# Quarter-block products inside one of seven half-block products, in the LSTM steps and in layer 3's second weights

## The chip, the cores and the metric

The kernel runs on one core of a Trainium2 chip. The core has five engines that run their own queues: TensorE (matrix products, written to the eight banks of PSUM), VectorE, ScalarE, GpSimd and SyncE. In the profile they are called PE (with PEld for TensorE's weight loads), DVE, ACT, POOL and SP. The metric is the device time of one execution in microseconds (us): 2432.9 us is the median of three runs of the kernel before.

## The reference

The input x has 128 batches of 64 nodes with 256 features, in float32. Four graph layers follow, each with a layer norm, a rectifier and a residual. Two of them matter here.

Layer 0 ends with four LSTMs. For p = 1 to 4 the 64 nodes are cut into windows of p nodes; an LSTM of p steps runs over every window, and its last state replaces the last node of the window:

```python
def step(carry, x_t):
    h, c = carry
    g = x_t @ Wih.T + h @ Whh.T + bias
    i, f, gg, o = jnp.split(g, 4, axis=-1)
    c = jax.nn.sigmoid(f) * c + jax.nn.sigmoid(i) * jnp.tanh(gg)
    h = jax.nn.sigmoid(o) * jnp.tanh(c)
    return ((h, c), None)
...
for p in range(1, MAX_SKIP + 1):
    nw = Tv // p
    wins = h[:, :nw * p, :].reshape(Bv * nw, p, Hd)
    last = _lstm_last(Wih[p - 1], Whh[p - 1], bih[p - 1], bhh[p - 1], wins)
    idx = jnp.arange(nw) * p + (p - 1)
    h = h.at[:, idx, :].set(last.reshape(Bv, nw, Hd))
```

Layer 3 is three graph convolutions with weights of 256x512 (W1), 512x1024 (W2) and 1024x256 (W3):

```python
h = jax.nn.relu(_slconv(x, adj, S, W1))
h = jax.nn.relu(_slconv(h, adj, S, W2))
return _slconv(h, adj, S, W3)
```

## The kernel before

All data are float32. The 8192 tokens are worked on in 16 groups (g) of 512. Layer 0 keeps its features in four tiles `hs`, transposed, and the residual x of the first four groups stays in the tiles `xs[0]` to `xs[3]` from the start of the kernel until layer 1.

Most large products are made by the scheme that is called `seven` (L172). Weights A and data B are each cut into 2x2 blocks. Eight block products would make the result; this scheme (Strassen's, in Winograd's form) needs seven, with sums of the blocks of A (`sums`, L219, s1 to s4) and differences of the blocks of B (`differences`, L210, t1 to t4). `sevens` (L243) names the pairs: product 1 is a11 b11, 2 is a12 b21, 3 is s4 b22, 4 is a22 t4, 5 is s1 t1, 6 is s2 t2, 7 is s3 t3. `seven` issues products 1, 5, 6, 7 into four banks (`ps`), copies products 1 and 5 to SBUF (`p1`, `p5`, L181 and L182 on ScalarE), adds product 6 to p1 and product 7 to p5 (L184 and L185 on VectorE), and returns `finish`. That one sums p1 and p5 on GpSimd (L189, the block 1,1), issues product 2 on top of product 1 (block 0,0 straight from the bank), product 3 on top of 5 (block 0,1, L195) and product 4 on top of 7 (block 1,0, L199). `end` applies the activation to each block.

In the LSTM (`next_step`, L701) a unit is n = nk x 32 columns in two blocks, so blocks of B are 256 columns wide for p = 1, 2 and 4 and 224 for p = 3. Contraction runs over x and h (the two rows of blocks, 256 features each, two chunks of 128), and a block of A holds 128 of the 256 rows of each gate. One step has two gate sets: i and g, then f and o. Each gate set is one `seven`; one of its products is 2 gates x 2 chunks = 4 matmuls (L592). Two units (`two`) are worked on in turn. The first step of a window (`first_steps`, L650) has no h and is made by `gate_set` too; step t = 1 and later are `next_step`. The pairs of units are counted by j; pair j = 2 of p = 4 is the last of the LSTM, and beside its steps the results are turned and stored to DRAM (`turn_nodes`, on SP), added to the residual by GpSimd's adding transfers (`add_turned`), and layer 1 begins with `ln_relu(xs[0], h)`. The weights' sums for one p are made by `blocks_of` (L736) on VectorE, at the first pair; `ss[1]` is s2.

In layer 3, `second_weights` (L1582) multiplies the mixed features (512) by W2 (1024 columns out): for q = 0 and 2 one `seven` each, whose products are 2 x 2 matmuls (L1599) of 256 columns. Both are started before either is finished. `s2s[1]` is s2 of W2, and `m1`'s differences are `ts`. The loop over g is at L1719. `third_weights` (L1627, L1649) has blocks of 128 columns.

The order within an engine's queue is not the program's order. The framework lists the instructions by priority, which is program order, and when it builds the kernel it plans when each one's inputs will be there; an instruction that is not expected to be ready is passed by a later one of the same engine that is. `tc.issue_after` keeps single instructions behind others. On the chip the queues run in the order so fixed, and wait on semaphores.

Of the kernel before, what the change touches and what calls it, by code (L numbers as in the profile page):

```python
# [39 lines left out]
def adj_preln_kernel(ctx: ExitStack, tc: tile.TileContext, x_in, adj, vec, bg0, bg1,  # L40
# [9 lines left out]
    def bank(shape=(P, 512)):  # L50
        return psp.tile(list(shape), F32, tag="ps", name="ps")
# [119 lines left out]

    def seven(products, banks, p1, p5, out, end, parts=lambda b: [b]):  # L172

        ps = banks
        for i, p in zip((1, 5, 6, 7), ps):
            products[i](p, True)  # L180
        nc.scalar.copy(p1, ps[0])  # L181
        copied = nc.scalar.copy(p5, ps[1])  # L182

        nc.vector.tensor_tensor(p1, p1, ps[2], ALU.add)  # L184
        added = nc.vector.tensor_tensor(p5, p5, ps[3], ALU.add)  # L185

        def finish():
            sums_on_pool.append(
                nc.gpsimd.tensor_tensor(out=out[1][1], in0=p1, in1=p5, op=ALU.add).ins  # L189
            )  # L190
            end(1, 1, None)
            products[2](ps[0], False)
            end(0, 0, ps[0])
            products[3](ps[1], False)
            nc.vector.tensor_tensor(out[0][1], p1, ps[1], ALU.add)  # L195
            end(0, 1, None)
            products[4](ps[3], False)
            for to, p, q in zip(*(parts(b) for b in (out[1][0], p1, ps[3]))):
                last = nc.vector.tensor_tensor(to, p, q, ALU.add)  # L199
                end(1, 0, None, to)  # L200
            return last.ins

        finish.behind = added.ins
        finish.copied = copied.ins
        return finish

    def each_behind(behind, i):
# [108 lines left out]
    with tc.tile_pool(name="lw", bufs=5) as lw:  # L316
# [242 lines left out]
        with tc.tile_pool(name="back", bufs=1, reuse_waits="tile") as back_pool, \  # L559
# [19 lines left out]
            def by_chunk(blocks):  # L579
                return [[b[:, c] for c in range(2)] for b in blocks]  # L580

            def gate_set(p, n, g, gates, w, bs):

# [16 lines left out]
                out = [[g[:, :, m, blk, 0:n] for blk in range(2)] for m in range(2)]  # L600
                p15 = lp.tile([P, 2, 2, 256], F32, tag="p15", name="p15")
                same = gates[0][1:] == gates[1][1:]
# [5 lines left out]
                def end(m, blk, ps, part=None):  # L608
# [8 lines left out]
                return seven(  # L617
                    {i: product(i) for i in range(1, 8)}, [bank((P, 2, 256))[:, :, 0:n] for _ in range(4)],
                    p15[:, 0, :, 0:n], p15[:, 1, :, 0:n], out, end,
                )  # L620
# [79 lines left out]

            def next_step(t, p, n, u, ws, last_sum=None):  # L701

# [12 lines left out]
                if last_sum is not None:  # L715
                    last_sum()
                b = (by_chunk([x1]) + [None], by_chunk([h1, h2]), by_chunk(ts))
                ig, fo = gate_tile(), gate_tile()
                gate_i, gate_g, gate_f, gate_o = (g[:, r, :, :, 0:n] for g in (ig, fo) for r in range(2))
                gate_set(p, n, ig, [(0, 0, AF.Sigmoid), (1, 2, AF.Tanh)], ws, [b] * 2)()  # L720
                nc.vector.tensor_tensor(gate_i, gate_i, gate_g, ALU.mult)
                gate_set(p, n, fo, [(0, 1, AF.Sigmoid), (1, 3, AF.Sigmoid)], ws, [b] * 2)()
                nc.vector.tensor_tensor(cell, cell, gate_f, ALU.mult)
# [12 lines left out]
            def blocks_of(p, wi, wh):  # L736
# [11 lines left out]

                make(range(3))
                ws = [by_chunk([wx[:, m], wm[:, m]]) for m in range(2)] + [by_chunk(ss)]  # L750
                return ws, lambda: make([3])

# [3 lines left out]
                w_next[0], lw.tile([P, 2, 1024], F32, tag="w", name="s"), copied_of[5:9]  # L756
            )
            for p, nk in ((1, 8), (2, 8), (3, 7), (4, 8)):
                n = nk * HB
# [6 lines left out]
                for j in range(0, len(units), 2):  # L766
                    two = [unit(p, *u, nk) for u in units[j : j + 2]]
                    first_steps(p, n, two, units[j : j + 2], w0)
                    if p > 1:
                        flush()  # L770
                        if j == 0:
                            ws, last_sum = blocks_of(p, wi, wh)
                    if j + 2 == len(units):
# [5 lines left out]
                        else:  # L779
# [8 lines left out]
                            nc.vector.tensor_tensor(ss[1], ss[0], wqk[0][0], ALU.subtract)  # L788
                            nc.vector.tensor_tensor(wdiff, wqk[0][0], wqk[1][0], ALU.subtract)
                    for t in range(1, p):  # L790
                        for i, u in enumerate(two):
                            stepped_before = stepped
                            stepped = next_step(
                                t, p, n, u, ws, last_sum if (j, t, i) == (0, 1, 0) else None
                            )
# [785 lines left out]

    def second_weights(m1, room):  # L1582

# [6 lines left out]
        ts = [tt[:, i] for i in range(4)]  # L1590
        last = differences(nc.vector, *act[0], *act[1], *ts)

        def products(q):
# [16 lines left out]
        for q in (0, 2):  # L1610
# [6 lines left out]
                    products(q), [bank((P, 2, HN)) for _ in range(4)], p1, p5, blocks,  # L1617
                    ends_in(blocks, AF.Relu),
                )
# [95 lines left out]

    AHEAD = 4
    a, finish_start = first_start()
    s3, scaled = None, None
    for g in range(NG + 1):  # L1719
# [32 lines left out]
        if g < NG:  # L1752
            h2, behind = second_weights(m1, h1)
            if g == 0:
# [71 lines left out]
```

## Time and profile before

| what | value |
|---|---|
| time, median of 3 runs (lowest to highest) | 2432.9 us (2431.64 to 2433.43) |
| the profiled execution: its own time, and its span from the first to the last instruction | 2432.54 us, 2430.8 us |
| granted TensorE clock in it | 0.999 |
| L592 (LSTM products), records of TensorE | 5012, from 156.9 us to about 1200 us |
| L1599 (layer 3, second weights), records of TensorE | 1792, from 1680.6 us to 2413 us |
| stretch 880 to 960 us (p = 4): busy us of 80 on PE, DVE, ACT, POOL | 80.0, 48.8, 35.3, 10.4 |
| stretch 640 to 720 us (p = 3): the same | 80.0, 49.2, 38.3, 10.7 |
| stretch 1680 to 1760 us (layer 3): the same | 80.0, 50.9, 26.8, 10.4 |

A row of the timeline gives start, length, engine, line and operation, what is written and read (by tile name), the shape, and how many like instructions were merged; in brackets stands how long the engine was idle before, and who ended it. The product of the seven can be told by its operands: "h,w" is product 1, "diff,s" are 5, 6 and 7, "state,w" is 2, "state,s" is 3 and "diff,w" is 4. A float32 matmul leaves two records on PE and two on PEld. Neighbouring matmuls overlap, so the length of a merged run is the starts' distance plus the latency of its last record.

### The profile page before, as it was taken

What the parts mean: (1) busy time and instruction counts of PE and PEld (TensorE: products, weight loads), DVE (VectorE), ACT (ScalarE), POOL (GpSimd) and SP (SyncE); (2) the same over time, 40 slices, a digit from 0 to 9 for tenths busy, and PEclk for the clock granted to TensorE, in tenths of its full rate; (3) what the DMA queues carried; (4) which work ended last, traced back from release to release, by engine and by line L of the source; (5) the groups of instructions that cost most, each with busy time, mean ns of one, the idle gap of its engine ahead of it and who ended that gap; (6) DMA issues with size and microseconds to landing.
All of it is one profiled execution on the core that took longest, in us unless ns stands there. A gap on an engine that the chain in (4) does not pass through costs nothing.

```text
span 2430.8 us, 46867 instructions
## 1 busy us (share of the span) xinstructions
PE 2409.7 (99%) x19648; PEld 2088.7 (86%) x19648; DVE 1546.7 (64%) x2829; ACT 1130.2 (46%) x2022; POOL 497.5 (20%) x445
## 2 busy tenths in 40 slices
PE   9999999999999999999999999999999999999999
PEld 6778888889999998888888867586988898999898
DVE  6768866666566575575599888576655445444543
ACT  4557755444445343353455565564343333333332
POOL 4432211111111111112224445123111111111100
PEclk9999999999999999999999999999999999999999
DMA  4200000001000000143246410010233100000000
GB/s 140 84 2 1 1 18 1 1 1 35 1 1 1 1 1 1 18 96 70 48 82 129 78 29 2 10 61 10 36 53 62 27 10 19 10 10 11 18 10 19
DMA packets 161587, 73.21 MB, mean 30 GB/s; under 512 B 104416, under 2 KB 157792, under 8 KB 161376
## 3 DMA queue, kind: packets, MB, share of 16 engines
q1 hardware_dynamic: 147984, 57.08, 9.5%
q0 software_dynamic: 12672, 12.58, 3.5%
q8 instruction: 154, 2.52, 0.4%
q10 hardware_dynamic: 720, 0.56, 0.1%
q14 instruction: 57, 0.47, 0.1%
HBM read 40.84 MB, written 20.97 MB: 25 GB/s over the span
## 4 chain that ended last, share of the span: by engine, by line
PE 92%; DVE 5%; ACT 2%; issue 1%; DMA 0%; POOL 0%; ACTq 0%; DVEq 0%; POOLq 0%
PE ps L592 41%; PE ps L1599 16%; PE ps L1649 8%; PE ps L1556 4%; PE ps L146 4%; PE ps L952 3%; PE ps L501 2%; PE ps L527 2%; PE ps L1326 2%; PE ps L878 2%; PE ps L911 2%; PE ps L1388 1%; PE ps L974 1%; PE ps L1670 1%; PE ps L1354 1%
## 5 line engine op out<-in xcount | busy, mean ns | idle before, releaser
L592 PE MATMUL ps<-diff,s 128*128 128x256 f32 (+1 forms) x1824 | 393.5, 371 | 0.9 <-DVE diff L713 0.9
L1599 PE MATMUL ps<-arena 128*128 128x256 f32 x1792 | 391.4, 380 | 0.0
L1599 PEld LDWEIGHTS ps<-arena 128*128 128x128 f32 x1792 | 338.9, 190 | 48.2 <-issue 2.0
L592 PEld LDWEIGHTS ps<-diff,s 128*128 128x128 f32 x1824 | 345.9, 190 | 33.8 <-issue 1.6
L606 ACT ACTIVATE gates<-gates,lbias 128x512 f32<-128x512 f32 (+5 forms) x426 | 244.1, 620 | 200.5 <-DVE gates L195 144.8
L189 POOL TENSOR_TENSOR gates<-p 128x512 f32<-128x512 f32 (+1 forms) x115 | 148.6, 1292 | 882.0 <-DVE p L185 831.1
L592 PE MATMUL ps<-h,w 128*128 128x256 f32 (+1 forms) x1028 | 241.0, 371 | 0.0
L592 PE MATMUL ps<-diff,w 128*128 128x256 f32 (+1 forms) x1040 | 238.7, 370 | 0.0
L189 POOL TENSOR_TENSOR arena<-arena 128x512 f32<-128x512 f32 (+1 forms) x80 | 91.1, 1139 | 613.7 <-DVE arena L185 601.4
L592 PEld LDWEIGHTS ps<-diff,w 128*128 128x128 f32 x1040 | 197.4, 190 | 18.2
L592 PEld LDWEIGHTS ps<-h,w 128*128 128x128 f32 x1028 | 195.0, 190 | 19.2 <-issue 0.5
L606 ACT ACTIVATE gates<-ps,lbias 128x256 f32<-128x256 f32 (+3 forms) x213 | 91.8, 477 | 247.2 <-PE ps L592 247.0
L239 ACT ACTIVATE arena<-arena 128x512 f32<-128x512 f32 x144 | 88.5, 628 | 250.4 <-POOL arena L189 163.1
L195 DVE TENSOR_TENSOR gates<-p,ps 128x512 f32<-128x512 f32 (+1 forms) x115 | 76.3, 664 | 114.3 <-PE ps L592 114.0
L1649 PE MATMUL ps<-arena 128*128 128x128 f32 x1280 | 148.4, 275 | 0.0
L1649 PEld LDWEIGHTS ps<-arena 128*128 128x128 f32 x1280 | 146.5, 192 | 0.9
L184 DVE TENSOR_TENSOR arena<-arena,ps 128x512 f32<-128x512 f32 (+1 forms) x80 | 48.2, 602 | 138.5 <-PE ps L1599 50.0
L195 DVE TENSOR_TENSOR arena<-arena,ps 128x512 f32<-128x512 f32 (+1 forms) x80 | 48.1, 602 | 125.5 <-PE ps L1599 57.6
L228 DVE TENSOR_TENSOR arena<-arena 128x512 f32<-128x512 f32 (+1 forms) x192 | 108.2, 597 | 21.9 <-ACT arena L239 20.2
L592 PE MATMUL ps<-state,w 128*128 128x256 f32 (+1 forms) x512 | 116.1, 370 | 0.9 <-ACT p L181 0.8
L184 DVE TENSOR_TENSOR p<-p,ps 128x512 f32<-128x512 f32 (+1 forms) x131 | 86.9, 663 | 47.4 <-PE ps L592 46.6
L199 DVE TENSOR_TENSOR gates<-p,ps 128x512 f32<-128x512 f32 (+1 forms) x115 | 76.6, 666 | 62.9 <-PE ps L592 62.4
(219 smaller groups left out, 4127.1 us busy)
## 6 DMA issues: line engine op xcount, KB each, us to landing
x<-in_x SPq DMA_DIRECT2D x19, 512.0 KB, 4.1
y<-turned SPq DMA_DIRECT2D x64, 128.0 KB, 3.7
v<-vt SPq DMA_DIRECT2D x128, 64.0 KB, 2.3
w<-in_wih SPq DMA_DIRECT2D x4, 1024.0 KB, 8.4
x_for_h<-in_x SPq DMA_DIRECT2D x8, 512.0 KB, 6.6
x<-y POOLq DMA_DIRECT2D x8, 512.0 KB, 6.3
x_for_h<-y POOLq DMA_DIRECT2D x8, 512.0 KB, 6.8
z<-w SPq DMA_DIRECT2D x64, 64.0 KB, 2.0
```

Source lines behind the costliest of these rows:

```text
L146: last = nc.tensor.matmul(pss[b][half * 64 : half * 64 + 64, c, t, :], lhsT=src[rows, t, col : col + 64], rhs=a2[rows, :], start=True, sto ...
L184: nc.vector.tensor_tensor(p1, p1, ps[2], ALU.add)
L189: nc.gpsimd.tensor_tensor(out=out[1][1], in0=p1, in1=p5, op=ALU.add).ins
L195: nc.vector.tensor_tensor(out[0][1], p1, ps[1], ALU.add)
L199: last = nc.vector.tensor_tensor(to, p, q, ALU.add)
L228: last = eng.tensor_tensor(out=s, in0=p, in1=q, op=op)
L239: nc.scalar.activation(o, o, func)
L592: nc.tensor.matmul(ps[:, r], lhsT=wc[:, j, :], rhs=bc, start=first and r == 0 and c == 0, stop=True, skip_group_check=True,)
L606: nc.scalar.activation(o, ps, func, bias=lbias[:, col : col + 1])
L1556: nc.tensor.matmul(ps[:, t, :], lhsT=w[:, t * P : (t + 1) * P], rhs=b, start=first and t == 0, stop=True, skip_group_check=True,)
L1599: nc.tensor.matmul(ps[:, r, :], lhsT=w[:, c, col : col + P], rhs=b[:, c, :], start=first and r == 0 and c == 0, stop=c == 1, skip_group_ch ...
L1649: nc.tensor.matmul(ps[:, t, :], lhsT=w[:, c, t * P : (t + 1) * P], rhs=b[:, c, :], start=first and t == 0 and c == 0, stop=c == 3, skip_gr ...
```

## The change

Product 6 (s2 t2) of a `seven` may be handed a `Split`. Then s2 and t2 are themselves cut into 2x2 blocks, quarter sums and quarter differences are made of them, and the product is made by the same scheme at half the size: seven products of quarters, each one matmul of half the columns, where there were four matmuls. Products 1, 5, 7 and 6 of the quarters go to the four quarters of the bank (`first`). `common` reads them: ScalarE copies quarter 0 to u, VectorE adds quarter 3 to u and quarters 1 and 2 to the last quarter of p1, and GpSimd adds u to the last three quarters of p1. Then `last` issues products 2, 3 and 4 of the quarters on top of quarters 0, 1 and 2 of the bank, and `rest` adds those to p1 on VectorE. The add of the whole of product 6 to p1 falls away.

The split is used in every `next_step` but those of p = 4, j = 2 (both gate sets, for p = 2, 3, 4), and in `second_weights` of the groups g = 3 to 15 (both q). The quarter sums of weights are made in `blocks_of` once for each p, and by `split_second` once at g = 2; the quarter differences are made once a step, and once a group.

The room for this in the LSTM is taken from the tiles of x0 to x3: they are freed after layer 0's first use, and x is loaded into them again from DRAM at the start of pair j = 2 of p = 4. In layer 3 two of these tiles are taken again after their groups are done. The banks and p15 of a gate set are laid out without a gap when n = 224.

```diff
     def seven(products, banks, p1, p5, out, end, parts=lambda b: [b], split=None):
...
         for i, p in zip((1, 5, 6, 7), ps):
-            products[i](p, True)
+            if i == 6 and split:
+                split.first(p)
+            else:
+                products[i](p, True)
         nc.scalar.copy(p1, ps[0])
         copied = nc.scalar.copy(p5, ps[1])
-
-        nc.vector.tensor_tensor(p1, p1, ps[2], ALU.add)
-        added = nc.vector.tensor_tensor(p5, p5, ps[3], ALU.add)
+        if split:
+            split.common(ps[2], p1)
+            split.last(ps[2])
+            added = nc.vector.tensor_tensor(p5, p5, ps[3], ALU.add)
+            split.rest(ps[2], p1)
+        else:
+            nc.vector.tensor_tensor(p1, p1, ps[2], ALU.add)
+            added = nc.vector.tensor_tensor(p5, p5, ps[3], ALU.add)
...
+    class Split:
+        def __init__(self, w, b, u):
+            (a11, a12), (_, a22), ss = w
+            (b11, _), (b21, b22), ts = b
+            self.m = (
+                None, (a11, b11), (a12, b21), (ss[3], b22), (a22, ts[3]),
+                (ss[0], ts[0]), (ss[1], ts[1]), (ss[2], ts[2]),
+            )
+            self.u = u
...
+        def issue(self, to, i, first=False):
+            w, b = self.m[i]
+            nc.tensor.matmul(to, lhsT=w, rhs=b, start=first, stop=True, skip_group_check=True)
+        def first(self, ps):
+            _, q = self.quarters(ps)
+            for k, i in enumerate((1, 5, 7, 6)):
+                self.issue(q[k], i, k == 0)
+        def last(self, ps):
+            _, q = self.quarters(ps)
+            for k, i in enumerate((2, 3, 4)):
+                self.issue(q[k], i)
+        def common(self, ps, to):
+            _, q = self.quarters(ps)
+            flat, t = self.quarters(to)
+            nc.scalar.copy(self.u, q[0])
+            nc.vector.tensor_tensor(self.u, self.u, q[3], ALU.add)
+            for k in (1, 2):
+                nc.vector.tensor_tensor(t[3], t[3], q[k], ALU.add)
+            h = self.u.shape[-1]
+            three = flat[:, h : 4 * h].rearrange("p (i n) -> p i n", n=h)
+            nc.gpsimd.tensor_tensor(
+                out=three, in0=three, in1=self.u.unsqueeze(1).to_broadcast([P, 3, h]), op=ALU.add
+            )
+        def rest(self, ps, to):
+            h = self.u.shape[-1]
+            (flat, _), (pf, _) = self.quarters(to), self.quarters(ps)
+            nc.vector.tensor_tensor(flat[:, 0 : 3 * h], flat[:, 0 : 3 * h], pf[:, 0 : 3 * h], ALU.add)
+    def split_differences(eng, t, ts):
...
+        eng.tensor_tensor(
+            out=ts[:, 0:3:2], in0=t[:, :, h:], in1=t[:, 0].rearrange("p (k n) -> p k n", n=h),
+            op=ALU.subtract,
+        )
+        eng.tensor_tensor(out=ts[:, 1], in0=b[1][1], in1=ts[:, 0], op=ALU.subtract)
+        eng.tensor_tensor(out=ts[:, 3], in0=b[1][0], in1=ts[:, 1], op=ALU.subtract)
...
                 if last_sum is not None:
                     last_sum()
+                splits = [None] * 2
+                if within:
+                    s2, sw, room = within
+                    half = n // 2
+                    tb = split_differences(
+                        nc.vector, ts[1],
+                        room[:, 0:2].rearrange("p a (i n) -> p (a i) n", i=2)[:, :, 0:half],
+                    )
...
-                gate_set(p, n, ig, [(0, 0, AF.Sigmoid), (1, 2, AF.Tanh)], ws, [b] * 2)()
+                gate_set(p, n, ig, [(0, 0, AF.Sigmoid), (1, 2, AF.Tanh)], ws, [b] * 2, splits[0])()
...
-                gate_set(p, n, fo, [(0, 1, AF.Sigmoid), (1, 3, AF.Sigmoid)], ws, [b] * 2)()
+                gate_set(p, n, fo, [(0, 1, AF.Sigmoid), (1, 3, AF.Sigmoid)], ws, [b] * 2, splits[1])()
...
                 make(range(3))
+                sw = split_sums[p % 2]
+                sums(
+                    nc.vector, *(ss[1][:, c, 2 * r : 2 * r + 2] for r in range(2) for c in range(2)),
+                    *(sw[:, i] for i in range(4)),
+                )
...
+            free = [xpool.tile([P, GT, D], F32, tag=f"x{g}", name=f"free{g}") for g in range(NK)]
+            split_sums = [f.rearrange("p a (i f) -> p a i f", f=P) for f in free[:2]]
...
+                    if p == 4 and j == 2:
+                        for g in range(NK):
+                            xs[g] = xpool.tile([P, GT, D], F32, tag=f"x{g}", name=f"x{g}")
+                            load_x(xs[g], g)
                     for t in range(1, p):
                         for i, u in enumerate(two):
                             stepped_before = stepped
                             stepped = next_step(
                                 t, p, n, u, ws, last_sum if (j, t, i) == (0, 1, 0) else None,
+                                None if p == 4 and j == 2 else (*within, free[2 + i]),
                             )
...
+    SPLIT_FROM = 3
+    within = None
...
-            h2, behind = second_weights(m1, h1)
+            h2, behind = second_weights(m1, h1, within)
+            if g == SPLIT_FROM - 1:
+                with tc.issue_after(behind):
+                    within = split_second()
```

## The prediction

> **What bounds the kernel.** I read the page's busy line and its chain that ended last first: they say which engine has to become shorter.
>
> ```profile
> span 2430.8 us, 46867 instructions
> ...
> PE 2409.7 (99%) x19648; PEld 2088.7 (86%) x19648; DVE 1546.7 (64%) x2829; ACT 1130.2 (46%) x2022; POOL 497.5 (20%) x445
> ...
> PE 92%; DVE 5%; ACT 2%; issue 1%; DMA 0%; POOL 0%; ACTq 0%; DVEq 0%; POOLq 0%
> ```
>
> TensorE is busy 99% of the span and is 92% of the chain. L592 (the LSTM's products) alone is 41% of that chain and L1599 (layer 3's second weights) 16%: the two places that the change touches. So time is gained only by less TensorE work, and every wait that the change puts on TensorE costs its full length.
>
> Next, the pace of TensorE by the width of a product, from the timeline. A float32 product appears as two matmul records, so the pace is per record: the run's length less one record's own latency (379, 353 and 275 ns, from the rows of single records), over the records but one.
>
> ```profile
> 904.77 5.34 PE L592 MATMUL ps<-diff,s 128*128 128x256 f32 x24
> ...
> 597.66 4.70 PE L592 MATMUL ps<-diff,s 128*128 128x224 f32 x24
> ...
> 1848.34 5.52 PE L1649 MATMUL ps<-arena 128*128 128x128 f32 x48
> ```
>
> That is (5.34 − 0.379)/23 = 215.7 ns at 256 columns, (4.70 − 0.353)/23 = 189.0 ns at 224, and (5.52 − 0.275)/47 = 111.6 ns at 128. From 256 to 224 columns the step is 26.7 ns, 0.834 ns per column. At that slope 128 columns would take 109.0 ns; the row says 111.6. Half as wide is thus a little more than half as long.
>
> **TensorE's own work.** One half-block product (number 6 of the seven) is four matmuls of full width, 8 records; it becomes seven quarter products, 14 records of half width.
>
> Count of the splits: an LSTM step has two gate sets, each with one split. p = 2 has 4 pairs of units × 1 step × 2 = 8 steps, p = 3 has 3 × 2 × 2 = 12, p = 4 has 3 × 2 = 6 in its first pair, as the second is excluded. That is 28 splits of 256 columns (p = 2 and 4) and 24 of 224 (p = 3). Layer 3 splits in groups 3 to 15, 13 × 2 = 26, at 256 columns.
>
> - 54 splits of 256 columns: 8 × 215.7 = 1726 ns become 14 × 111.6 = 1562 ns, 163 ns less each: **−8.8 us**.
> - 24 splits of 224: before, 8 × 189.0 = 1512 ns. After, 14 records of 112 columns, which no row shows. The bounds are the 128-column pace, 14 × 111.6 = 1562 ns (+50 ns each, +1.2 us in all), and the column slope carried on, 111.6 − 16 × 0.834 = 98.3 ns, 1376 ns (−136 ns each, −3.3 us). I take +1.2: the 128-column row lies above its own slope, which is what a floor under the record would look like, and it is the nearest row.
>
> The two say −7.6 us with a range of −12.1 to −7.6. Every record has its own weight load, 14 in place of 8 now, and at 128 columns the loads fill the time as well: L1649's 1280 loads are busy 146.5 us, 114 ns each.
>
> [...]
>
> **The new wait.** The last three quarter products add into the bank whose first four must have been read: by one ScalarE copy (u), one VectorE add into u and two into the last quarter of p1. In the first gate set of a step that fits:
>
> ```profile
> 927.21 1.89 PE L592 MATMUL ps<-h,w 128*128 128x256 f32 x8
> 928.94 5.34 PE L592 MATMUL ps<-diff,s 128*128 128x256 f32 x24
> 929.62 1.23 DVE L721 TENSOR_TENSOR gates<-gates 128x1024 f32<-128x1024 f32 x1 [1.52 <-ACT gates L606]
> 930.87 0.59 ACT L182 COPY p<-ps 128x512 f32<-128x512 f32 x1 [0.87 <-PE ps L592]
> 932.66 0.69 DVE L184 TENSOR_TENSOR p<-p,ps 128x512 f32<-128x512 f32 x1 [1.82 <-PE ps L592]
> ```
>
> Products 5, 6, 7 are the x24. With the split, 5 ends at 928.94 + 1.73 = 930.67, the four quarters at 931.56, product 7 at 933.29. Prices of the reads: a VectorE add from a bank takes 683 ns at 512 columns and 420 at 256 (rows of L184), so 0.29 us at 128 and 0.55 at 384; a ScalarE copy 0.58 and 0.37 (L181), so 0.26 at 128. A reader starts some 0.25 us after the last record's end by pace (L184 at 932.66 against 932.39). So u is copied 931.8 to 932.1, VectorE adds until 933.0, and product 7 still runs until 933.3: no wait, by 0.3 us. VectorE has nothing else there.
>
> The second gate set is different:
>
> ```profile
> 941.03 5.34 PE L592 MATMUL ps<-diff,s 128*128 128x256 f32 x24
> 942.30 1.23 DVE L724 TENSOR_TENSOR state<-state,gates 128x1024 f32<-128x1024 f32 x1
> 943.62 1.06 ACT L625 ACTIVATE gates<-state 128x1024 f32<-128x1024 f32 x1
> 944.71 1.23 DVE L627 TENSOR_TENSOR state<-gates 128x1024 f32<-128x1024 f32 x1 [1.18 <-ACT gates L625]
> 948.37 1.64 DVE L714 TENSOR_TENSOR diff<-state,diff 128x512 f32<-128x512 f32 x1
> ```
>
> The quarters end at 943.65, just as ScalarE goes into the tanh of L625 until 944.68; behind it VectorE has L627 until 945.94. The reads then end near 946.6, and product 7 ends at 945.38: 1.2 us late, if the three are next in TensorE's queue. Behind them wait products 2, 3, 4, and behind those the next step. They need not be next: the order of a queue is planned at build by when inputs are expected, and the trace shows this planning at 323.5 and 523.2 us, where product 2 ("state,w") runs before 6 and 7. Product 2 needs only the copy of p1, long done, and lasts 1.73 us, which covers 1.2. Bounds: 0, or 26 × 1.2 = 31 us. I take **+0.8 us**, some tenths in a few sets.
>
> **The rest of the readers.** Per split VectorE loses one add of 0.68 and gains 3 × 0.29 + 0.55 = 1.42: +0.74. The quarter differences are 0.42 (row of L228 at 256) + 2 × 0.28 by the same halving = 0.98, once per step or group, 39 times. In all 78 × 0.74 + 39 × 0.98 = 96 us of VectorE, about 2.5 us per LSTM step of 24.2, in which it is busy 14 of 24 (48.8 of 80 us in the stretch 880 to 960). It hides under TensorE, which is 80.0 of 80 there. GpSimd's added sum of 384 columns (1.28 and 0.83 at 512 and 256, so 1.05) hides likewise, though not for VectorE: L714 above takes 1.64 us beside GpSimd's L189, 0.69 without it. If cover failed, a step's VectorE work would still be under 18 of 24 us. p1 is complete later by about 1 us, as its last add must follow the late three; products 2 and 3 have 3.5 us in between, and the unit's next step starts after the other unit's 12 to 24 us.
>
> **Where VectorE is already late.** After the first steps of some pairs TensorE waits for differences:
>
> ```profile
> 525.03 1.89 PE L592 MATMUL ps<-state,s 128*128 128x256 f32 x8
> 526.45 0.68 DVE L713 TENSOR_TENSOR diff<-state,diff 128x512 f32<-128x512 f32 x1
> 527.28 3.69 PE L592 MATMUL ps<-diff,s 128*128 128x256 f32 x16 [0.36 <-DVE diff L713]
> ```
>
> Here 0.8 us is lost (523.2 and 527.3), at 588 another 0.8, at 790 and 794 1.1. The change puts in VectorE's queue, ahead of these differences, four quarter sums of weights (4 × 0.42 = 1.66 us, at the first pair of p = 2, 3, 4) and behind them 0.98. L713, L714, the other unit's differences and product 6 are queued behind. Bounds: 0, since 7, 2 and 3 can go first, and 3 × 2.64 + 2 × 0.98 = 9.9 us. I take **+1.2 us**, a little under half of the 2.7 us that these three places lose now, since TensorE has other products at hand in most of them.
>
> **The moved loads.** Groups 0 to 3 of x are loaded a second time: four issues on SP at the start of the second pair of p = 4, ahead of the "turned" stores. They wait for the last split of the first pair (about 1036 us); the first adding transfer into them comes two steps on. A 512 KB load lands in 4.1 us. SP's queue carries stores for 28 us there, but no TensorE work waits for those until layer 1, at 1200. Cost 0; without that cover 2.1 MB at the 140 GB/s of the first slice are 15 us.
>
> **Sum.** −8.8 + 1.2 + 0.8 + 1.2 = −5.6 us: span 2430.8 to 2425.2. The profiled execution took 2432.54, 1.7 around its span and 0.4 below the median; the same off the median 2432.9 gives **2427.3 us**.
>
> **Rivals.**
> - *Given back.* The reads are late by 0.2 us in the 26 second gate sets (5.2 us), or the boundaries take half of their 9.9. Then −7.6 + 5.2 + 1.2 = −1.2, 2431.7 us. For it: 0.3 us of margin is the best place; the trace has planned orders that came out 0.3 to 0.8 us late on the same engines. Against: product 2 is always at hand.
> - *Slower.* In the second gate set the planner puts the three right behind product 7, and TensorE stands 1.2 us behind L625 and L627 in each: −7.6 + 31 + 1.2 = +24.6, about 2457.5 us. From 0.24 us a set the saving is gone, from 0.43 the kernel is over 0.2% slower ((7.6 − 1.2 + 4.9)/26). For it: ScalarE and VectorE rows above; against: the orders at 323.5 and 523.2.
> - *Narrow records run by their columns.* At 98.3 ns p = 3 gives −3.3 instead of +1.2: −10.1, 2422.8 us. For it: the slope from 256 to 224; against: the 128 row above its slope.
>
> **How the numbers follow.** Forecast 0.50, narrow records 0.08, given back 0.25, slower 0.17. About 0.2% (4.9 us) is what a measurement of this kernel can tell from no change: faster than 2428.0 is the forecast and the narrow records, 0.58; within is given back, 0.25; slower 0.17. The range 2421.5 to 2437 holds all but the slow case and 0.03. The forecast's own range is 2424 to 2429.
>
> **What would show it.** TensorE's records rise by 78 × 6 to 20116; the quarter records pace 111.6 ns, at 112 columns too. Idle TensorE before the new quarter line, released by VectorE or ScalarE, shows the new wait: under 2 us in all if I am right, 31 if the slow rival is. The gaps at 523, 588 and 790 us stay within a microsecond or so of now. I am wrong if the order puts waiting quarters first, or if narrow weight loads are slower beside wide products.

## The result: 34 us slower, most of it in layer 3

The changed kernel takes 2467.32 us (median of 4 runs, 2464.92 to 2469.77) against 2433.06 us (4 runs beside them, 2431.64 to 2433.43). The ratio is 1.0142, 95% interval 1.0124 to 1.016. The prediction was 2427.3 us with a range of 2421.5 to 2437: wrong in sign.

The page of the changed kernel, the lines that answer to those shown of before. The profiled execution took 2469.77 us, around a span of 2468.0.

```profile
span 2468.0 us, 48426 instructions
...
PE 2417.8 (98%) x20116; PEld 2096.9 (85%) x20116; DVE 1638.2 (66%) x3196; ACT 1146.2 (46%) x2100; POOL 577.5 (23%) x523
...
PE 88%; DVE 9%; ACT 1%; issue 1%; POOL 1%; DVEq 0%; ACTq 0%; POOLq 0%
```

The records are the 20116 that were counted in advance. VectorE is busy 92 us more (96 were worked out). TensorE's share of the chain of waits fell from 92 to 88%, and VectorE's rose from 5 to 9%: TensorE now waits for VectorE more often. The chain says which engine, and neither where nor how much; that comes from cutting the span into stages, at the first TensorE record of each stage's own line.

| us, profiled executions | start | LSTM | attention | to layer 3's second weights | layer 3 |
|---|---|---|---|---|---|
| before | 156.9 | 1044.9 | 222.6 | 256.2 | 746.1 |
| after | 159.3 | 1045.1 | 229.1 | 254.3 | 775.9 |

"Attention" begins with the first product of "hT,w" (L952 before, L1057 after), the next stage with the first of L878 (L983), "layer 3" with the first of L1599 (L1727) and ends with the last record of TensorE. Of the 37 us between the spans 29.8 are in layer 3, and 6.5 in the attention, which the change does not touch. The start differs by 2.4 us, but kernels with the same code there took 156.8 to 159.3.

The rows that were to show the steps of the prediction come next, from the timeline. First the pace of the quarter products, L233 in the changed kernel, at 112 columns and at 128 (product 6 of an LSTM gate set each):

```profile
600.72 0.37 PE L233 MATMUL ps<-diff,s 128*128 128x112 f32 x2
600.93 0.83 PE L233 MATMUL ps<-free,free 128*128 128x112 f32 x6
601.60 1.69 PE L664 MATMUL ps<-diff,s 128*128 128x224 f32 x8
...
934.00 0.39 PE L233 MATMUL ps<-diff,s 128*128 128x128 f32 x2
934.22 0.83 PE L233 MATMUL ps<-free,free 128*128 128x128 f32 x6
934.89 1.89 PE L664 MATMUL ps<-diff,s 128*128 128x256 f32 x8
```

Eight records last from 934.00 to 934.89 at 128 columns and from 600.72 to 601.60 at 112: 0.89 and 0.88 us, 110 to 111 ns a record. Over the whole run, where TensorE does not wait, a quarter record is followed after 111 or 112 ns at both widths. Only the first one behind a wide product is shorter, 96 ns at 112 columns and 109 at 128, and the wide record behind the last one is as much longer (205 ns in place of 189, 218 in place of 216). Against 128 columns, 112 gained nothing.

Next the second gate set of an LSTM step, the place that the slow rival feared:

```profile
946.82 1.89 PE L664 MATMUL ps<-diff,s 128*128 128x256 f32 x8
948.55 1.89 PE L664 MATMUL ps<-state,w 128*128 128x256 f32 x8
950.44 0.46 PE L233 MATMUL ps<-diff,s 128*128 128x128 f32 x2
```

The records of product 2 (state,w) stand ahead of the last three quarter products, as at 323.5 and 523.2 us before. The reads end late (VectorE's second L251 starts at 950.01, while product 7 ends at 948.55), and product 2 covers that but for 0.17 us.

And the place that was not looked at. The waits of TensorE, summed over the run (released by whom, total, times, longest):

```profile
PE ps L233 <- DVE arena L251: 22.6, 12, 2.7
...
PE ps L1104 <- issue: 4.3, 3, 2.0
```

L251 are the two adds that read quarters 1 and 2 of product 6's bank; writing to "arena" they are layer 3's. (L1104 is a line of the attention; it comes back below.) One of the waits on L251, TensorE's timeline in layer 3:

```profile
2028.45 3.72 PE L1727 MATMUL ps<-arena 128*128 128x256 f32 x16
2032.01 0.38 PE L233 MATMUL ps<-arena 128*128 128x128 f32 x2
2032.23 0.91 PE L233 MATMUL ps<-free,free 128*128 128x128 f32 x6
2032.98 1.89 PE L1727 MATMUL ps<-arena 128*128 128x256 f32 x8
2037.58 0.62 PE L233 MATMUL ps<-arena 128*128 128x128 f32 x2 [2.71 <-DVE arena L251]
```

Products 1 and 5 (x16), four quarters, product 7 (x8), and then the last three stand next in the queue. Nothing was put between. VectorE in the same microseconds, with ScalarE's copy u (L248) among its rows:

```profile
2030.33 1.41 DVE L285 TENSOR_TENSOR arena<-arena 128x512 f32<-128x512 f32 x2
2031.65 0.42 DVE L268 TENSOR_TENSOR free<-arena 128x256 f32<-128x256 f32 x1
2031.99 0.42 DVE L93 BATCH_NORM_STATS2 st<-x_for_h 128x6 f32<-128x256 f32 x1
...
2033.18 0.27 ACT L248 COPY free<-ps 128x128 f32<-128x128 f32 x1 [0.39 <-PE ps L233]
...
2035.69 0.16 DVE L99 SCALAR_TENSOR_TENSOR nmr<-mv,rstd 128x4 f32<-128x4 f32 x1 [0.90 <-POOL rstd L97]
2035.77 0.95 DVE L297 TENSOR_TENSOR arena<-arena 128x256 f32<-128x256 f32 x2
2036.63 0.28 DVE L249 TENSOR_TENSOR free<-free,ps 128x128 f32<-128x128 f32 x1
2036.83 0.60 DVE L251 TENSOR_TENSOR arena<-arena,ps 128x128 f32<-128x128 f32 x2
```

The quarters are done at 2032.9 and ScalarE's copy u at 2033.45, but VectorE comes to its first read, L249, at 2036.63. In front of it stand the differences of this group, the layer norm's statistics for the group after next (L93 to L99, among them 0.90 us in which VectorE waits for GpSimd) and four sums for the next group's first product (L297). In the second set of the same group VectorE has nothing in front: L249 starts right behind its copy, and TensorE does not wait.

```profile
2044.83 0.29 DVE L249 TENSOR_TENSOR free<-free,ps 128x128 f32<-128x128 f32 x1 [5.12 <-ACT free L248]
```

Eleven of the twelve waits are in the first sets of groups 3 to 13 (the twelfth, 0.22 us, is in the second set of group 3); groups 14 and 15, which have no layer norm ahead of them, have none.

The same rows could have been read before the change. The kernel before at the same place, TensorE's run of both sets and then VectorE:

```profile
2012.59 24.44 PE L1599 MATMUL ps<-arena 128*128 128x256 f32 x112
2015.79 1.40 DVE L93 BATCH_NORM_STATS2 st<-x_for_h 128x6 f32<-128x256 f32 x4
...
2019.09 0.16 DVE L99 SCALAR_TENSOR_TENSOR nmr<-mv,rstd 128x4 f32<-128x4 f32 x1 [0.91 <-POOL rstd L97]
2019.17 0.95 DVE L228 TENSOR_TENSOR arena<-arena 128x256 f32<-128x256 f32 x2
2020.03 0.68 DVE L184 TENSOR_TENSOR arena<-arena,ps 128x512 f32<-128x512 f32 x1
```

The set's first product starts at 2012.59, so by the pace product 6 ends at 2012.59 + 24 x 0.2157 = 2017.8 and product 7 at 2019.5; yet L184, the reader of product 6, starts at 2020.03. It already came 2.3 us behind the product's end, and that cost nothing while no TensorE work needed its bank: the 112 records run on without a gap.

After this wait, one of the longest, the granted clock falls as well. The windows around the wait (length; busy time and records of PE, PEld, DVE, ACT, POOL; granted clock, DMA share, GB/s):

```profile
2024.00:2037.58 13.58, 10.87 (x244) 9.24 (x243) 11.21 (x31) 5.46 (x10) 1.37 (x3) 1.00 0.13 41
2037.58:2041.50 3.92, 3.92 (x13) 3.42 (x14) 1.01 (x2) 0.38 (x1) 2.29 (x2) 0.56 0.01 4
2041.50:2048.00 6.50, 6.50 (x38) 5.93 (x37) 2.01 (x5) 1.69 (x4) 1.35 (x2) 1.00 0.00 0
```

Layer 3's account, by the distance of two starts less the pace of the first record: idle ahead of quarter products 27.8 us, idle ahead of L1727 records up from 3.4 to 8.8 (of the 5.4 us more 4.3 lie in three stretches at half clock, and 1.0 at two places where nothing releases TensorE), and 26 splits saving 163 ns each. 27.8 + 5.4 - 4.2 = 29.0 of the 29.8 us.

### The profile page after: what moved, and what is told of

Same layout as the page of the kernel before. It is cut to its first block, busy times and chain, and to the rows that moved or that the text cites. A ratio compares the mean times of both kernels' runs of the same rounds, so it can differ in the third digit from the quotient of the medians.

```text
span 2468.0 us, 48426 instructions
## 1 busy us (share of the span) xinstructions
PE 2417.8 (98%) x20116; PEld 2096.9 (85%) x20116; DVE 1638.2 (66%) x3196; ACT 1146.2 (46%) x2100; POOL 577.5 (23%) x523
## 4 chain that ended last, share of the span: by engine, by line
PE 88%; DVE 9%; ACT 1%; issue 1%; POOL 1%; DVEq 0%; ACTq 0%; POOLq 0%
PE ps L664 37%; PE ps L1727 12%; PE ps L1777 8%; PE ps L233 5%; PE ps L1661 4%; PE ps L146 3%; PE ps L1057 3%; PE ps L570 2%; PE ps L596 2%; PE ps L1431 2%; PE ps L983 2%; PE ps L1016 2%; PE ps L1079 1%; PE ps L1493 1%; DVE arena L285 1%
## 5 line engine op out<-in xcount | busy, mean ns | idle before, releaser
L1727 PE MATMUL ps<-arena 128*128 128x256 f32 x1584 | 359.3, 383 | 1.0 <-issue 1.0
L1727 PEld LDWEIGHTS ps<-arena 128*128 128x128 f32 x1584 | 298.6, 192 | 42.3 <-issue 3.1
L664 PE MATMUL ps<-diff,s 128*128 128x256 f32 (+1 forms) x1408 | 317.3, 372 | 0.0
L664 PEld LDWEIGHTS ps<-diff,s 128*128 128x128 f32 x1408 | 263.1, 190 | 24.9
L664 PE MATMUL ps<-h,w 128*128 128x256 f32 (+1 forms) x1028 | 241.5, 371 | 0.0
L664 PE MATMUL ps<-diff,w 128*128 128x256 f32 (+1 forms) x1040 | 239.9, 370 | 0.0
L664 PEld LDWEIGHTS ps<-diff,w 128*128 128x128 f32 x1040 | 196.8, 190 | 17.9
L664 PEld LDWEIGHTS ps<-h,w 128*128 128x128 f32 x1028 | 194.8, 190 | 19.1 <-issue 0.5
L254 POOL TENSOR_TENSOR p<-p,free 128x384 f32<-128x384 f32 (+1 forms) x52 | 54.6, 1050 | 417.5 <-DVE p L251 417.5
L1777 PEld LDWEIGHTS ps<-arena 128*128 128x128 f32 x1280 | 146.5, 192 | 0.9
L203 DVE TENSOR_TENSOR arena<-arena,ps 128x512 f32<-128x512 f32 (+1 forms) x80 | 48.1, 601 | 127.3 <-PE ps L1727 59.0
L297 DVE TENSOR_TENSOR arena<-arena 128x512 f32<-128x512 f32 (+1 forms) x192 | 109.3, 601 | 21.6 <-ACT arena L308 20.2
L664 PE MATMUL ps<-state,w 128*128 128x256 f32 (+1 forms) x512 | 118.9, 370 | 0.3 <-ACT p L184 0.2
L664 PE MATMUL ps<-state,s 128*128 128x256 f32 (+1 forms) x512 | 117.6, 369 | 0.0
```

The costliest lines, as they stand in the source:

```text
L297: last = eng.tensor_tensor(out=s, in0=p, in1=q, op=op)
L664: nc.tensor.matmul(ps[:, r], lhsT=wc[:, j, :], rhs=bc, start=first and r == 0 and c == 0, stop=True, skip_group_check=True,)
L1727: nc.tensor.matmul(ps[:, r, :], lhsT=w[:, c, col : col + P], rhs=b[:, c, :], start=first and r == 0 and c == 0, stop=c == 1, skip_group_ch ...
L1777: nc.tensor.matmul(ps[:, t, :], lhsT=w[:, c, t * P : (t + 1) * P], rhs=b[:, c, :], start=first and t == 0 and c == 0, stop=c == 3, skip_gr ...
```

## The experiments

The stages of all kernels, beside before and after above:

| us | start | LSTM | attention | to second weights | layer 3 |
|---|---|---|---|---|---|
| LSTM's split alone | 157.2 | 1045.0 | 226.8 | 254.3 | 747.5 |
| layer 3's split alone | 158.2 | 1044.9 | 222.5 | 254.6 | 773.2 |
| layer norm behind the reads | 158.3 | 1045.0 | 226.0 | 254.3 | 746.8 |
| layer 3's last three later | 157.6 | 1045.1 | 226.1 | 254.3 | 746.2 |
| L99 alone behind the reads | 159.2 | 1045.1 | 227.1 | 254.3 | 760.6 |
| before, with 41 idle matmuls | 165.7 | 1044.9 | 226.8 | 254.3 | 747.2 |
| layer 3 alone, last three later | 157.0 | 1044.9 | 222.6 | 254.6 | 745.6 |
| last three later, no split in p = 3 | 157.1 | 1043.0 | 224.6 | 254.3 | 745.7 |
| the same, the LSTM's last three later too | 156.8 | 1042.4 | 224.2 | 254.2 | 745.4 |

### One half of the change at a time

```diff
-    SPLIT_FROM = 3
+    SPLIT_FROM = NG + 2
```

> The split stays in the LSTM steps and is taken out of layer 3's second weights. Theory (the loss is layer 3's: TensorE waits there for VectorE's reads in the first of the two sets): about 2433 to 2442 us, the upper end if the extra 6.5 us in the attention stage and 2.4 us before the LSTM come with the LSTM's part; the LSTM stage itself within 1 us of 1042.9 us. Rival (the second gate sets of the LSTM carry the loss): 2455 us or more.

Measured: 2436.64 us (11 runs), ratio 1.0016, interval 1.0007 to 1.0025. Layer 3 is back at 747.5 us, and without its splits it has no wait for L251. The LSTM is where it was before (1045.0 against 1044.9; within 1 us of 1042.9 was expected): its part of the change gains nothing, and something in the attention costs 4.2 us.

The other half, with the LSTM's split, its sums and the second load of x taken out:

```diff
-                                None if p == 4 and j == 2 else (*within, free[2 + i]),
+                                None,
```

> The split stays in layer 3 alone; no second load of x, no quarter sums in the LSTM. Theory: layer 3 from its first group on takes some 776 us in place of 746, so 2460 to 2465 us, and the wait for the adds that follow the quarters is again 22 us or so. Rival (LSTM): 2428 to 2438 us.

Measured: 2460.27 us (4 runs), ratio 1.0112, interval 1.0098 to 1.0126. Layer 3 takes 773.2 us, the attention 222.5 as before. TensorE's first wait is

```profile
PE ps L233 <- DVE arena L251: 20.8, 12, 2.7
```

So the two losses are apart: the large one belongs to layer 3's split, the small one to the LSTM's.

### Is it the work ahead on VectorE?

The layer norm of the group after next is kept behind the two reads of L251 in the first set, in place of an earlier point; all of it still runs.

```diff
             for k in (1, 2):
-                nc.vector.tensor_tensor(t[3], t[3], q[k], ALU.add)
+                self.read = nc.vector.tensor_tensor(t[3], t[3], q[k], ALU.add)
...
-                with tc.issue_after(behind):
+                with tc.issue_after(read.ins if read else behind):
                     scaled = ln_scale(xs[g + 2])[:2]
```

> As the changed kernel, but the layer norm's statistics for the group after next stand on VectorE behind the first set's reads of the quarters, not ahead of them. Theory (the reads come late because statistics, and a wait for GpSimd's power in their midst, stand ahead of them in VectorE's queue): the wait falls from 22.6 to under 8 us, no half clock follows, 2440 to 2450 us. Rival (VectorE has too much work in the stage, whatever its order): the wait stays at 15 us or more, 2458 us or more.

Measured: 2436.46 us (10 runs), ratio 1.0013, interval 1.0004 to 1.0022; layer 3 746.8 us, no half clock in it, and of the 22.6 us of waiting is left

```profile
PE ps L233 <- DVE arena L251: 1.6, 2, 1.4
```

The same VectorE work, only in another order, gives back 29 us in layer 3; the time is even 3.5 us below the range that was expected. It is the place in the queue that cost, not the 92 us that VectorE has more to do.

Which part of that work? Only L99, the instruction that waits for GpSimd's power, goes behind the reads:

```diff
-                    scaled = ln_scale(xs[g + 2])[:2]
+                    scaled = ln_scale(xs[g + 2], (lambda: read) if read else None)[:2]
```

> The changed kernel, with one instruction of layer 3's normalisation (line 99, which waits for GpSimd's power) behind the two adds that read product 6's bank in the first set of gates of second_weights; the statistics of lines 93 to 96 and the sums of line 297 stay ahead of them. It divides the 20 to 27 us of waiting. Theory A, work queued ahead on VectorE: the statistics alone are 2 to 2.5 us of VectorE in each of eleven groups, so with the wait for GpSimd gone (0.90 us in the group at 2035 us) the wait of the quarter products on line 251 falls by about 0.9 us a group, from 22.6 to 10 to 14 us, and the half-clock stretches vanish; layer 3 takes 758 to 766 us against 775.9. Rival B, the wait for GpSimd is all of it: line 251's wait falls under 4 us, as with all of the normalisation moved (1.6 us). Rival C, the wait for GpSimd is nothing: the wait stays at 20 us or more.

Measured: one run, 2452.45 us; layer 3 760.6 us, no half clock in it. The wait now goes by two names, as the order in VectorE's queue is another:

```profile
PE ps L233 <- DVE nmr L99: 9.7, 9, 1.6
...
PE ps L233 <- DVE arena L251: 2.7, 3, 1.7
```

Together 12.4 us, within theory A's 10 to 14; rival B's 4 and rival C's 20 are both out. VectorE waiting for GpSimd, 0.9 us a group, and the half clock that follows the longer idles account for about half of the loss (layer 3: 15.3 us). The other half goes with the statistics, as the run before this one shows, which moved them too (13.8 us more); the sums of L297 stayed ahead of the reads there, and hardly any wait was left.

### The cure on TensorE's side

The last three quarter products and `rest` go from `seven` to `finish`, behind product 2, in layer 3 alone:

```diff
-            split.last(ps[2])
+            if not split.later:
+                split.last(ps[2])
             added = nc.vector.tensor_tensor(p5, p5, ps[3], ALU.add)
-            split.rest(ps[2], p1)
+            if not split.later:
+                split.rest(ps[2], p1)
...
         def finish():
+            later = split and split.later
+            if later:
+                products[2](ps[0], False)
+                split.last(ps[2])
+                split.rest(ps[2], p1)
             sums_on_pool.append(
...
-            products[2](ps[0], False)
+            if not later:
+                products[2](ps[0], False)
```

> As the changed kernel, but in layer 3 the last three quarter products and their add are issued in the finish, behind product 2, so that the first set's stand behind all of the second set's first four products. Theory (a wait that TensorE need not have stood in): the wait is gone in layer 3, whose span becomes 742 to 744 us, 30 us less than in the changed kernel; 2433 to 2440 us. Rival (the reads are what is slow, and block what follows wherever they stand): 2455 us or more.

Measured: 2435.88 us (11 runs), ratio 1.0013, interval 1.0004 to 1.0022. No wait on these adds is left. In TensorE's timeline the quarters (L242 in this kernel) run on without idle time:

```profile
2018.97 0.91 PE L242 MATMUL ps<-free,free 128*128 128x128 f32 x6
2019.71 5.34 PE L1736 MATMUL ps<-arena 128*128 128x256 f32 x24
2024.90 0.38 PE L242 MATMUL ps<-arena 128*128 128x128 f32 x2
...
2025.79 3.62 PE L1736 MATMUL ps<-arena 128*128 128x256 f32 x16
2029.24 0.38 PE L242 MATMUL ps<-arena 128*128 128x128 f32 x2
```

Layer 3 takes 746.2 us, not the 742 that the saved records would make of 746.1: 1.6 us of small idle times ahead of quarter products remain, and the idle times where nothing releases TensorE ("issue") are 6.2 us in seven places of layer 3, where before had 3.6 in five. With this and without the LSTM's split:

> Layer 3's split alone, with its last three quarter products behind product 2 instead of behind product 7; the LSTM as before. Theory A, with the wait of line 251 gone the split is worth what its records say: 26 sets by 8 x 215.7 - 14 x 111.6 = 163 ns are 4.2 us, less 1.6 us of waits that are left behind quarter products and up to 2.5 us of fetch stalls that depend on where blocks of 256 instructions end: layer 3 at 742 to 747 us against 746.1, attention at 222.6 as before, the time 2428 to 2434 us. Rival B, the split of layer 3 costs something beside the wait: layer 3 above 749 us, the time over 2436.

Measured: 2432.48 us (11 runs) against 2432.18, ratio 1.0, interval 0.9991 to 1.0009; layer 3 745.6 us. Theory A holds, and the split in layer 3, freed of its wait, comes out at no measurable gain.

### What the attention lost

The idle times of TensorE in the middle of runs of equal small products, with "issue" as their releaser, were set against the number of the instruction in TensorE's stream (weight loads, matmuls and semaphore events). In the attention of the changed kernel the three long ones, which end at 1231.19, 1262.13 and 1432.70 us, all lie at 192 or 193 more than a multiple of 256; so do the ones at L146 in layer 3, before and after. Ahead of each of the three ends a packet of the instruction queue landed, at 1229.71, 1260.66 and 1431.41 us, 1.3 to 1.5 us earlier. Before, that queue moved 154 packets of 16 KB (2.52 MB), one for every 256.9 of TensorE's 39565 instructions (39565 / 154):

```profile
q8 instruction: 154, 2.52, 0.4%
```

The LSTM's split adds 677 instructions (624 loads and matmuls, 53 semaphore events), twice 256 and 165 more, so these places move to other products. To test this without the change, the kernel before gets 41 idle matmuls more at its start, 164 instructions:

```diff
-            keep_busy(7)
+            keep_busy(48)
```

> The kernel before with 41 more idle matmuls at its start and nothing of the change. They add 164 instructions to TensorE's stream, which moves the numbering of all that follows to that of the kernel with the LSTM's split alone (677 more, and 677 is 513 more than 164, two blocks of 256 and one). Theory A, the stalls of TensorE in the attention stage of layer 1 come from where blocks of 256 instructions end among its small matmuls: the attention stage takes 225.5 to 229.5 us as in the kernels with the LSTM's split (226.0 to 229.1), with idle of 1 to 2 us ahead of a k,q matmul at the same place in the stage. Rival B, they come from the LSTM's split itself (its tiles in the place of x, the second load of x): the attention stage takes 222.6 us as before. The first stage gets up to 9 us longer by the matmuls themselves.

Measured: one run, 2444.78 us; the attention takes 226.8 us, as with the LSTM's split, although no part of the change is there. The start is longer by 8.8 us, by the idle matmuls. TensorE's timeline at one stage of the attention, first before, then padded:

```profile
1225.59 1.14 PE L999 MATMUL ps<-k,q 64*64 64x64 f32 x63
1226.65 1.99 PE L974 MATMUL ps<-w,hT 128*128 128x256 f32 x8
```

```profile
1234.37 1.04 PE L999 MATMUL ps<-k,q 64*64 64x64 f32 x58
1237.03 0.33 PE L999 MATMUL ps<-k,q 64*64 64x64 f32 x5 [1.62 <-issue]
1237.29 1.99 PE L974 MATMUL ps<-w,hT 128*128 128x256 f32 x8
```

A run of 64 equal products, which took one stretch before, is cut after the 58th by 1.62 us of nothing. In the changed kernel it is cut at the same record (1228.18, x58, then 1.97 us). Theory A holds: 4.2 us of the attention (226.8 against 222.6) came with an edit that only moves the instructions' numbers, as they come with the LSTM's split. The changed kernel loses another 2.3 us there; its idle time before 1231.19 is followed by a stretch at half clock, worth some 1.7 us, which the kernel with the LSTM's split alone does not have.

### The steps of three, and a version that beats both

The split is taken out of p = 3, whose quarter records are 112 columns wide, on top of layer 3's last three placed later:

```diff
-                                None if p == 4 and j == 2 else (*within, free[2 + i]),
+                                None if p == 3 or (p == 4 and j == 2) else (*within, free[2 + i]),
```

> The changed kernel with the last three quarter products of layer 3 behind product 2, and without the split in the LSTM's steps of three (24 sets with quarter records of 112 columns). Theory A, a quarter record of 112 columns takes as long as one of 128 (111.6 ns), so the split of these sets only cost: the LSTM falls from 1045.1 to 1043.0 to 1043.6 us; layer 3 stays at 745 to 747; attention is 222 to 227 us by where the blocks of 256 instructions fall; the time 2430 to 2435.5 us. Rival B, the records of 112 columns were no loss: the LSTM stays at 1045 us and the time at 2435 to 2437.

Measured: 2430.35 us (11 runs), ratio 0.9992, interval 0.9983 to 1.0001. The LSTM falls to 1043.0 us, 2.1 less than with those 24 sets split, as theory A has it. The records are 1.2 us of it (50 ns in each of 24 sets). Most of the rest is idle time of TensorE ahead of its products in the LSTM, which falls from 6.5 to 5.8 us.

Last, the LSTM's own last three go behind product 2 by the program too, not only by the planned order:

> As the kernel without the split in the steps of three, but in the LSTM's steps of two and four too the last three quarter products stand behind product 2. Theory A, the 3.5 us that TensorE still idles ahead of quarter products in the LSTM are the reading of product 6's bank by ScalarE and VectorE, so four records of product 2 (0.86 us) in between take most of it away: idle ahead of quarter products in the LSTM 0.5 to 1.5 us, the LSTM 1040.5 to 1042.5 us against 1043.0, the time 2427.5 to 2430.5 us. Rival B, the three are needed for the set's next sum (p1, which GpSimd adds to p5 behind line 261), and later products come later to the next step: what is saved ahead of quarter products comes back ahead of the next step's products (line 673's waits grow from 1.1 us), the LSTM stays within 0.5 us of 1043.0 or gets longer.

Measured: 2429.26 us (11 runs) against 2432.92, ratio 0.9987, interval 0.9978 to 0.9996. This is faster than both kernels, if by 0.13%. The LSTM takes 1042.4 us, within theory A's range, but its idle time ahead of quarter products fell only from 3.5 to 2.8 us, not to 0.5 to 1.5: the planned order had put product 2 first in most sets already. Rival B's price did not appear: TensorE's waits for the next step's differences are the same 0.9 us in both kernels.

## Why the prediction was wrong, point by point

- **The step that failed** is "The new wait". It works out the reads' lateness for the two gate sets of an LSTM step, takes +0.8 us with a bound of 26 LSTM sets, and never looks at `second_weights`, where 26 of the 78 splits are. Layer 3 stood in the sum with its saving alone. There, in 11 first sets, VectorE reaches the reads so late that TensorE stands for 1.1 to 2.9 us, 24.2 us in all. With what is lost ahead of the other quarter products that is 27.8 us, and 5.4 more ahead of the wide products, most of it at half clock, where the sum had 0. The order put waiting quarters first, which the prediction had named as a sign that it is wrong.
- The paragraph on the rest of the readers covered VectorE's added work by the busy share (14 of 24 us, 48.8 of 80). That share was right, and it hid the added work; but a share says nothing of the queue in front of one instruction. The rows of before at 2015 to 2020 us had the answer: the reader of product 6 came 2.3 us behind the product's end, in a stage in which the table has VectorE idle for over a third of the time (busy 50.9 of 80).
- The slow rival (0.17, 2457.5 us) had the mechanism, the three standing right behind product 7 with VectorE late, and nearly the time. That the time is near is luck: its 31 us are 26 waits of 1.2 in the LSTM, and the trace has 11 of 1.1 to 2.9 in layer 3. It had the wrong place: in the LSTM's second gate sets the planned order put product 2 in between, as the forecast argued; in layer 3's first sets it put nothing there. In the kernel with the last three later, the second set's products follow product 7 there without idle time, so work was at hand. Why the plan left it behind was not tried.
- **TensorE's own work** was right: 20116 records, and 111 to 112 ns for each at 112 columns as at 128. The trace settles what the slope left open: records of 112 columns that follow one another took no less than the row at 128, where the slope would have had 98.3 ns. Only the first one behind a wide product is shorter, 96 ns, and its gain is lost again behind the last (205 ns in place of 189). The narrow-records rival is out.
- **The LSTM** was mis-sized. Its terms (28 x 163 ns = 4.6 saved, 1.2 for p = 3, 0.8 and 1.2 of waits) make -1.4 us; measured is +0.2. The idle time ahead of quarter products is 5.6 us, against which that ahead of L664 fell by 2.3 (3.1 to 0.8), so 3.3 where 2.0 were priced. The 0.3 us that are left are in no single place.
- **The moved loads** cost nothing that can be seen: with the padded kernel the attention lost its 4.2 us without them.
- **Not in the sum at all**: the attention's 4 to 6.5 us. That unrelated code may shift by its instruction count was not among the rivals.

## What to carry to other kernels

When a change makes TensorE wait for a reader, look up in the trace of before when that reader starts today, at every place the change touches: a reader that is late for free can become a wait (here 2.3 us late before, 24.2 us of waits after), and the engine's busy share does not show it (50.9 of 80 us). Then put independent products between the write and its reuse in the program itself, or move the other work on the reader's queue behind it. Look up at which width a narrower product stops being shorter (here 128 columns and 112 both went at 111 to 112 ns a record), as a scheme that trades columns for records stops paying there (without the 24 splits at 112 the LSTM took 2.1 us less).

## What the runs showed of the hardware

**TensorE idle at fixed places of its instruction stream.** At a fixed place in every 256 instructions (192 or 193 more than a multiple) TensorE stood still for 0.6 to 2.2 us (distance of two starts less the pace) at some of those places that fell into runs of 64x64 products, of which 64 go by in 1.0 to 1.2 us, or shortly behind them. Ahead of the three long ones in the attention a 16 KB packet of the instruction queue landed 1.3 to 1.5 us before TensorE went on. In the LSTM's wide products no such idle time is seen, before or after. By the padded kernel, 4.2 us of this kernel's attention hang on where these places fall.

**The clock fell after some idle times of 1.5 to 2.9 us.** Of the four idle times of 2.87 to 2.88 us ahead of quarter products in the changed kernel (2.71 in the timeline's brackets) three were followed by 3.4 us at half clock (the window above shows 0.56), and so was one of 2.17 us in the attention (1.97 in brackets) and one of 1.54 us at 1444 us before (1.37 in brackets, behind which small products ran with further gaps of up to 0.25). One such stretch cost about 1.6 us: the stage with the one of before takes 256.2 us, and 254.6 in the kernel with layer 3's split alone, where the same idle time was not followed by one (granted clock 1.00 from 1445.4 to 1448.9 us there, 0.51 from 1445.5 to 1449.0 before). In the clock's own records the four stretches of the changed kernel last 3.413 us each and begin at 1232.20, 2037.74, 2187.93 and 2338.12 us, which are 236, 44 and 44 such lengths apart. If the span is divided into steps of that length from these starts, the three long idle times that were followed by half clock lie each within one step, and the fourth, which ends at 1988.14, falls into two, 1.3 and 1.6 us. By the idle time within one step (brackets), 2.71, 2.71, 2.71 and 1.97 us in the changed kernel were followed by half clock and 1.91 (at 1938.69) and less were not; before, 1.44 at 1444 us was. So these runs fix no length that is enough, and whether the division into two steps is what spared the fourth they do not settle.
